# Mixing stage of a fused convolution and Laplace layer: a third tile for the mixed rows, an earlier start of the weights, another form of the exponentials, and another order of the evictions

## The chip, the cores and the metric

The kernel runs on one core of a Trainium2 chip. The metric is the device time of one execution in microseconds; three executions of the kernel before are shown below, and one more was recorded by the profiler. TensorE (PE) multiplies matrices, VectorE (DVE), ScalarE (ACT) and GpSimd (POOL) work on tiles in on-chip memory, and SyncE (SP) issues transfers between that memory and the chip's main memory. Each engine takes its own instructions strictly in the order in which they were written.

## What is computed

The input `x` has 16 images of 16 channels of 256 by 256 points, in 32-bit floats. Two layers follow one another, each of the form x + layer(group norm of x):

```python
x = x + _L0_conv_ref(_gn(x), L0_conv_weight)      # a 3x3 circular convolution
x = x + _L1_conv_ref(_gn(x), L1_conv_ty, ...)     # a Laplace layer
```

The second layer takes the two-dimensional Fourier transform `alpha` of its input. For every frequency pair (o, x) a 16 by 16 matrix of complex numbers mixes the channels, and the result is transformed back. The matrices come from poles and residues:

```python
A = 1.0 / (omega1[:, None, None, None] - weights_pole1[None])
Bm = 1.0 / (omega2[:, None, None, None] - weights_pole2[None])
S = jnp.einsum('ikpq,oikp,xikq->oxik', weights_residue, A, Bm)
output_residue1 = jnp.einsum('biox,oxik->bkox', alpha, S)
```

A second, transient part sums exponentials exp(pole * t) along both axes, with residues `output_residue2` made from `alpha`, `A` and `Bm`. The output is the real part of both parts plus the layer's input.

## The kernel before

The work has four stages, and TensorE is busy in nearly all of each: the convolution (to about 574 us of the profile), the forward transform along lines and columns (to 1193), the mixing of the channels (to 1860) and the transforms back with the output (to the end). The change touches the third stage most; the fourth stage takes over its memory.

In the mixing stage a *group* g (0 to 31) is a set of four frequencies of one axis with all those of the other, and each group has four *places* n. The spectrum lies in main memory as `aD`; the mixed result goes to main memory as `yD`. Per place, in the order in which the loop near line 1222 writes it:

- `sums` (line 1032): 32 small matmuls of the weights `w` with the table `ct` make the mixing matrices of the *next* group into two tiles `ps_s`.
- `spread` (lines 1049 and 1052) brings them to `sg`: for each of the two tiles ScalarE copies one half and VectorE shuffles one half. There are two `sg` tiles, one of this group and one of the next.
- four times `mix` (line 1120): 16 matmuls of `sg` with the spectrum in `abd` make a tile `ps_mix`, which is copied into a quarter of the tile `yt` (line 1233), the first three by ScalarE and the last by VectorE. In a place where `late` is set, VectorE takes two of the four.
- SP's transfers: at place 1 two loads of the next group into `abd01` (line 1102), then always four `store`s of 128 KB each from `yt` to `yD` (line 1134), then the rest of the loads of the next group: at place 1 two more into `abd01` (256 KB each), at places 2 and 3 four of 128 KB each into `abd2` and `abd3` (line 1107), at place 0 none.
- one step of `weights` for the group after next: three steps on VectorE, and with the last the spread of `v` to `w` on POOL (line 930).
- one step of the exponentials `make_exps` (lines 1172 to 1212): for each of 16 pairs of columns POOL works out an angle and brings it into the range of the sine, ScalarE takes exponential and sine, POOL multiplies and folds them, and SP stores the result to `eD`. A pair has seven steps.

There is one `abd` tile per place pair (`abd01`) or place (`abd2`, `abd3`), so a load of the next group waits until the mixes of this one have read it. There are two `yt` tiles, so the copies of one place wait until the stores of the place before the last have landed. All these loads and stores go through SP's one queue. The order of every engine is that of the program text (`manual_schedule`): nothing is reordered.

In group 31 the rows of frequency 0 are taken apart again (`unmix_first`, lines 1139 to 1157), by four loads and four stores of `yD`. Then the fourth stage begins: POOL issues loads of `et`, `ey`, `inv` and of rows 0 to 119 of the mixed result `yk`, SP loads rows 120 to 127 (line 1283), and POOL combines rows into `u` (lines 1325 and 1329), the operand of the first transform back (line 1361).

On-chip memory is laid out by hand: pools in the order in which the stage opens them, with tiles of the fourth stage over those of the third.

Of the kernel before, what the change touches and what calls it, by code (L numbers as in the profile page):

```python
# [9 lines left out]
FP = mybir.dt.float32  # L10
AF = mybir.ActivationFunctionType
# [5 lines left out]
B = 16  # L17
# [7 lines left out]
def conv_then_laplace_kernel(ctx: ExitStack, tc: tile.TileContext, a: dict, out: bass.AP):  # L25
# [25 lines left out]

    later_loads = []

    def const(name, shape):
        t = cp.tile(shape, FP, name=name, tag=name)
        later_loads.append((t, a[name]))
        return t

    cols = const("cols", [P, 24])
    kmask = const("kmask", [P, C])  # L60
    fold2 = const("fold2", [P, 2, 64])
    o2 = cp.tile([P, B, 2, 16], FP, name="o2", tag="o2")
    proj = cp.tile([P, 2, B, 16, 2], FP, name="proj", tag="proj")
    jmat = cp.tile([P, 3, P], FP, name="jmat", tag="jmat")

    def pitched(name, rows, row, *split):

# [27 lines left out]

    ptab = ExitStack()
    tp = ptab.enter_context(tc.tile_pool(name="tables", bufs=1))
    vmr = tp.tile([P, 2, B, C], FP, name="vmr", tag="vmr")


# [54 lines left out]
    own = m16[:, 0:C:2]  # L155
    load_consts()
    halves[1] = [load_x(1, h) for h in range(2)]
    nc.sync.dma_start(out=jmat, in_=a["jmat"])
    ones = tp.tile([P, P], FP, name="ones", tag="ones")
    nc.vector.memset(ones, 1.0)  # L160
    tiny = wp.tile([P, 8], FP, name="tiny", tag="tiny")
# [557 lines left out]
    def pool(stage, name, bufs=1, **kw):  # L719
        return stage.enter_context(tc.tile_pool(name=name, bufs=bufs, reuse_waits="tile", **kw))  # L720
# [174 lines left out]
    def weights(g):  # L895

        shape = [P, 32, 4]
        u = up["u" if g else "u0"].tile([P, 4, 32, 4], FP, name="u", tag="u")  # L900
        w, den, e, f = (u[:, j] for j in range(4))
        pr2, pre, pim = (prU[:, j].unsqueeze(2).to_broadcast(shape) for j in range(3))
        nc.vector.tensor_tensor(
            w,
            omg[:, g].unsqueeze(1).to_broadcast(shape),
            pims.unsqueeze(2).to_broadcast(shape),
            ALU.subtract,
        )
        nc.vector.tensor_tensor(den, w, w, ALU.mult)
        nc.vector.tensor_tensor(den, den, pr2, ALU.add)  # L910
        yield
        nc.vector.reciprocal(den, den)

        nc.vector.scalar_tensor_tensor(e, w, m1, pre, ALU.mult, ALU.add)
        nc.vector.scalar_tensor_tensor(f, w, nm0, pim, ALU.mult, ALU.add)
        yield
        v = up["v"].tile([P, 32, 2, 4], FP, name="v", tag="v")
        nc.vector.tensor_tensor(v[:, :, 0], e, den, ALU.mult)
        nc.vector.tensor_tensor(v[:, :, 1], f, den, ALU.mult)
        if g == 0:  # L920
            yield
        wt = wp.tile([P, 4, 8, 32], FP, name="w", tag="w")
        v2 = v.rearrange("p a r s -> p a (r s)")
        w4 = wt.rearrange("p a k (i m) -> p (a k) i m", i=4)
        if g == 0:
            for i in range(4):
                nc.scalar.activation(w4[:, :, i], v2, AF.Copy, scale=m4[:, i : i + 1])
            return wt
        full = [P, 32, 4, 8]
        nc.gpsimd.tensor_tensor(  # L930
            w4,
            v2.unsqueeze(2).to_broadcast(full),
            m4.unsqueeze(1).unsqueeze(3).to_broadcast(full),
            ALU.mult,
        )
        return wt
# [44 lines left out]
    ptab.close()  # L981


    yp = pool(p2, "yt", 2)
    g0 = pool(p2, "sg0")
    a0 = pool(p2, "abd0")
    wp = pool(p2, "w", 2)
    ep = pool(p2, "exps")
    up["u"] = pool(p2, "u")
    a1 = pool(p2, "abd2")  # L990
    zp = pool(p2, "between")
    tp = pool(p2, "ct")
    a2 = pool(p2, "abd3")
    g1 = pool(p2, "sg1")
# [10 lines left out]
        z.tile([P, 4, 4, 16, B], FP, name=f"abd{j}", tag=f"abd{j}") for j, z in ((2, a1), (3, a2))  # L1005
    ]

    zp.tile([P, 384], FP, name="between", tag="between")
    ct = tp.tile([P, 4, 8, N], FP, name="ct", tag="ct")
    nc.sync.dma_start(out=ct, in_=cD)  # L1010
    def next_step(steps, w):
# [28 lines left out]

    swap = [p ^ 4 for p in range(32)]

    def spread(n, *pairs):


        for odd in range(2):
            for to, src in pairs:
                k = 4 * n + 2 * odd
                nc.scalar.activation(to[..., k : k + 2], src[odd], AF.Copy, scale=nsgn)  # L1049
            for to, src in pairs:  # L1050
                k = 4 * n + 2 * (1 - odd)
                nc.vector.stream_shuffle(to[..., C + k : C + k + 2], src[1 - odd], swap)  # L1052

    def first_sums():
# [27 lines left out]
            load(0, jq)  # L1082
        return sg, w1

    def finish_projections():


        for ro in range(2):
            ps = pm.tile([P, B, 16], FP, name="ps_o", tag="ps_mix")
            nc.tensor.matmul(ps, lhsT=jmat[:, 0], rhs=accs[:, ro], start=True, stop=False)  # L1090
            nc.tensor.matmul(ps, lhsT=jmat[:, 2 - ro], rhs=accs[:, 1 - ro], start=False, stop=True)
            nc.vector.tensor_copy(o2[:, :, ro], ps)

    def load(g, jq, rows=range(4)):

# [65 lines left out]
    def make_exps(which):  # L1161


        pl = ep.tile([P, C, 2], FP, name="s_pl", tag="s_pl")
        nc.sync.dma_start(out=pl, in_=a[f"pole_e{which + 1}"])
        t = ep.tile([P, N], FP, name="s_t", tag="s_t")
        nc.sync.dma_start(out=t, in_=a[("ty", "tx")[which]].to_broadcast([P, N]))
        sign, phase, turns = (cols[:, 2 + 3 * which + j : 3 + 3 * which + j] for j in range(3))
        pim = ep.tile([P, C], FP, name="s_pim", tag="s_pim")
        for _ in range(4):  # L1170
            yield
        nc.gpsimd.tensor_scalar(pim, pl[:, :, 1], sign, None, ALU.mult)
        for q in range(8):
            th = ep.tile([P, 2, N], FP, name="s_th", tag="s_th")
            rn = ep.tile([P, 2, N], FP, name="s_rn", tag="s_rn")
            tmp = ep.tile([P, 2, N], FP, name="s_tmp", tag="s_tmp")
            ex = ep.tile([P, 2, N], FP, name="s_ex", tag="s_ex")
            for j in range(2):
                i = 2 * q + j
                nc.gpsimd.tensor_scalar(th[:, j], t, pim[:, i : i + 1], None, ALU.mult)  # L1180
            nc.gpsimd.tensor_scalar(rn, th, 1.0 / (2 * PI), turns, ALU.mult, ALU.add)
            magic = 1.5 * 2.0**23
            nc.gpsimd.tensor_scalar(rn, rn, magic, None, ALU.add)
            nc.gpsimd.tensor_scalar(rn, rn, magic, None, ALU.subtract)
            yield
            c1 = 6.28125
            c2 = float(np.float32(1.93500518798828125e-3))
            c3 = 2 * np.pi - c1 - c2
            for c in (c1, c2, c3):
                nc.gpsimd.tensor_scalar(tmp, rn, float(c), None, ALU.mult)  # L1190
                nc.gpsimd.tensor_tensor(th, th, tmp, ALU.subtract)
                if c == c2:
                    yield
            nc.gpsimd.tensor_scalar(th, th, phase, 3.1415925, ALU.add, ALU.min)
            nc.gpsimd.tensor_scalar(th, th, -3.1415925, None, ALU.max)
            for j in range(2):
                i = 2 * q + j
                nc.scalar.activation(ex[:, j], t, AF.Exp, scale=pl[:, i, 0:1])
            yield True
            yield  # L1200
            nc.scalar.activation(th, th, AF.Sin)
            yield True
            nc.gpsimd.tensor_tensor(th, th, ex, ALU.mult)
            for op, eo in ((ALU.add, 0), (ALU.subtract, 1)):
                nc.gpsimd.tensor_tensor(
                    ex[:, :, eo * P : eo * P + P], th[:, :, 0:P], th[:, :, N - 1 : P - 1 : -1], op
                )
            yield
            for o in range(2 - which):
                nc.sync.dma_start(  # L1210
                    out=eD[which][o, :, 2 * q : 2 * q + 2].rearrange("p i e t -> p i (e t)"),
                    in_=ex,
                )
            yield
# [1 line left out]
    p2.enter_context(tc.manual_schedule())  # L1216
    accs = yp.tile([P, 2, B, 16], FP, name="accs", tag="yt")
    ahead, wt = first_sums()
    finish_projections()
    unmix = None  # L1220
    exps, late = chain(make_exps(0), make_exps(1)), None
    for g in range(32):
        sg, w_now = ahead, wt
        steps = weights(g + 2) if g < 30 else iter(())
        ahead = new_sg(g + 1) if g < 31 else None
        for n in range(4):
            evict = sums(n, w_now) if ahead is not None else []
            yt = yp.tile([P, 2, 4 * B, 16], FP, name="yt", tag="yt")
            if evict:
                spread(n, (ahead, [z.rearrange("p q n -> p n q") for z in evict]))  # L1230
            for m in range(4):
                o, src = mix(4 * n + m, sg, yt)
                (nc.vector.tensor_copy if m >= (2 if late else 3) else nc.scalar.copy)(o, src)  # L1233
            if n == 1 and g < 31:
# [3 lines left out]
                load(g + 1, n, (2, 3) if n == 1 else range(4))  # L1238
            if n == 1 and unmix is not None:
                next(unmix, None)  # L1240
            wt = next_step(steps, None) or wt
            late = g and next(exps, None)
        if g == 30:
# [210 lines left out]
def _constants():  # L1454
# [45 lines left out]
    cols[:, 6], cols[:, 7] = np.where(even, np.pi / 2, 0), np.where(even, 0.25, 0)  # L1500
    cols[:, 9] = np.where(even, -1.0, 0.0)
    cols[:, 12:16] = p[:, None] // 8 % 4 == np.arange(4)
    cols[:, 17] = p > 0
    cols[:, 16] = -cols[:, 17]
    cols[:, 19] = np.where(p > 0, 1.0, 0.5)
# [104 lines left out]
```

## Time and profile before

| what | value |
|---|---|
| three executions | 2618.83, 2619.7, 2624.65 us; median 2619.7 |
| the profiled execution | 2623.94 us, its span (first to last instruction) 2622.1 us |
| mean granted TensorE clock | 0.986 |
| busy share of the span | PE 94%, weight loads 72%, VectorE 76%, ScalarE 55%, POOL 49% |
| stage 3, 1219 to 1836 us: PE, VectorE, ScalarE, POOL busy | 586.1, 499.8, 400.4, 383.5 of 617 us |
| stage 3: transfers | 16 DMA engines busy 0.77 of the time, 223 GB/s |
| stage 4, 1860 to 2622 us: PE busy | 735.6 of 762 us |

The profile lists for each group of instructions the line, the engine, the operation, the names of the tiles that it writes and reads, its shape and count, then the busy time and the mean duration of one in nanoseconds, then the idle time of the engine just before such instructions and the event that ended most of it. An arrow `<-` reads "from" between tiles and "was ended by" in waits. A number after L is a line of the kernel. A chain of waits follows the work back from an end: each row is a piece of time and what was going on in it. SPq stands for SP's sequencer, and "issue" for time in which nothing that the profile shows was waited for.

### The profile page before, as it was taken

The numbers are of one execution on the slowest core, as the hardware profiler recorded it, in microseconds if no ns is written. First come the engines' busy times: TensorE is split into PE (matmuls) and PEld (weight loads), VectorE is DVE, ScalarE is ACT, GpSimd is POOL, SyncE is SP. The second block draws the span as 40 slices with busy tenths as digits, with TensorE's granted clock in tenths as the row PEclk, the third lists the DMA queues.
The fourth block names the chain that finished last, engine by engine and source line by source line (L and its number), as shares of the span: only waits on it lengthen the run. The fifth ranks groups of instructions, "written<-read, shape, count | busy, mean of one in ns | idle before, by whom it ended". The sixth has DMA issues, their size and how long they took to land.

```text
span 2622.1 us, 84262 instructions
## 1 busy us (share of the span) xinstructions
PE 2468.6 (94%) x35314; PEld 1885.3 (72%) x35314; DVE 1980.8 (76%) x3772; ACT 1432.6 (55%) x2599; POOL 1290.5 (49%) x1179
## 2 busy tenths in 40 slices
PE   5998999989999999998999999999799999999998
PEld 2444455567777777775878778788688888888887
DVE  7777788848888888887877878887276676667666
ACT  2565566666666666665666656666244444444443
POOL 1333378433333333333666645766555565555553
PEclk9999999989999999999999999999899999999999
DMA  7888878854655655655777777777988888888884
GB/s 274 276 279 282 294 270 294 297 211 177 240 195 209 242 220 194 245 225 190 225 229 214 226 225 222 222 227 228 253 302 289 291 292 279 299 289 287 291 287 174
DMA packets 318011, 653.17 MB, mean 249 GB/s; under 512 B 49174, under 2 KB 163990, under 8 KB 305728
## 3 DMA queue, kind: packets, MB, share of 16 engines
q1 hardware_dynamic: 316464, 640.57, 72.4%
q8 instruction: 278, 4.55, 0.7%
q0 software_dynamic: 896, 3.02, 0.4%
q10 hardware_dynamic: 272, 4.19, 0.4%
q14 instruction: 101, 0.83, 0.1%
HBM read 368.15 MB, written 280.36 MB: 247 GB/s over the span
## 4 chain that ended last, share of the span: by engine, by line
PE 58%; DVE 7%; DMA 4%; SPq 3%; ACT 3%; POOL 2%; issue 1%; ACTq 0%; DVEq 0%; POOLq 0%
PE ps_mix L1120 9%; PE ps_y L777 9%; PE ps_y L785 8%; PE ps_p L1361 7%; PE ps_f L1385 7%; PE ps_f L1386 7%; PE ps_x L820 5%; DMA yD<-yt 4%; PE ps_s L1032 2%; SPq L1134 2%; PE ps_h L1345 2%; PE psd L805 1%; DVE r L1394 1%; DVE ol L1396 1%; DVE ol L1397 1%
## 5 line engine op out<-in xcount | busy, mean ns | idle before, releaser
L1120 PE MATMUL ps_mix<-abd,sg 128*64 128x128 f32 x8192 | 482.2, 276 | 39.4 <-DMA yD<-yt 16.6
L1120 PEld LDWEIGHTS ps_mix<-abd,sg 128*64 128x64 f32 x8192 | 451.9, 138 | 92.9 <-ACT yt L1233 55.7
L1325 POOL TENSOR_TENSOR u<-yk 128x512 f32<-128x512 f32 (+1 forms) x268 | 358.2, 1369 | 314.7 <-PE ps_p L1361 249.1
L305 PE MATMUL ps_conv<-xt,wc 32*32 32x512 f32 x12288 | 445.6, 602 | 36.0 <-issue 26.1
L305 PEld LDWEIGHTS ps_conv<-xt,wc 32*32 32x32 f32 x12288 | 251.1, 103 | 217.6 <-issue 127.0
L793 ACT ACTIVATE t<-ps_y,vmr 128x384 f32<-128x384 f32 x512 | 297.1, 580 | 161.1 <-PE ps_y L785 161.1
L1052 DVE STREAM_SHUFFLE sg<-ps_s 128x512 f32<-128x512 f32 (+1 forms) x264 | 329.1, 1316 | 0.0
L777 PE MATMUL ps_y<-tabE,vq 128*128 128x256 f32 x1024 | 313.2, 388 | 11.0 <-DVE vq L766 9.4
L785 PE MATMUL ps_y<-tabO,vq 128*128 128x256 f32 x1024 | 305.9, 380 | 0.0
L275 POOL TENSOR_TENSOR pair<-pair,far 128x1024 f32<-128x1024 f32 x64 | 151.7, 2370 | 304.1 <-DVE pair L272 207.7
L1385 PE MATMUL ps_f<-pt,inv 128*128 128x256 f32 x1008 | 300.4, 380 | 0.0
L1386 PE MATMUL ps_f<-hs,ey 128*128 128x256 f32 x1008 | 299.8, 379 | 0.0
L1361 PEld LDWEIGHTS ps_p<-inv,u 128*128 128x128 f32 x2048 | 268.9, 193 | 35.4 <-POOL u L1329 10.9
L1389 DVE TENSOR_TENSOR r<-ps_f,q 128x256 f32<-128x256 f32 x256 | 107.0, 418 | 241.9 <-ACT q L1388 241.9
L1361 PE MATMUL ps_p<-inv,u 128*128 128x128 f32 x2048 | 276.2, 278 | 9.8 <-POOL u L1329 9.7
L1049 ACT ACTIVATE sg<-ps_s,mcol 128x512 f32<-128x512 f32 (+1 forms) x264 | 179.3, 689 | 192.2 <-DVE sg L1052 117.1
L777 PEld LDWEIGHTS ps_y<-tabE,vq 128*128 128x128 f32 x1024 | 189.6, 191 | 87.5 <-ACT q L833 51.2
L1388 ACT COPY q<-ps_f 128x256 f32<-128x256 f32 x256 | 95.4, 373 | 274.7 <-PE ps_f L1386 250.4
L1363 ACT COPY pt<-ps_p 128x512 f32<-128x512 f32 x256 | 151.5, 592 | 134.9 <-PE ps_p L1361 134.9
L765 POOL TENSOR_TENSOR vq<-vf 128x512 f32<-128x512 f32 x64 | 81.4, 1272 | 291.6 <-DVE vf L769 281.5
L785 PEld LDWEIGHTS ps_y<-tabO,vq 128*128 128x128 f32 x1024 | 195.4, 191 | 26.9
L1233 ACT COPY yt<-ps_mix 128x512 f32<-128x512 f32 x352 | 184.1, 592 | 55.8 <-DMA yD<-yt 42.2
(237 smaller groups left out, 3993.6 us busy)
## 6 DMA issues: line engine op xcount, KB each, us to landing
xt<-in_x SPq DMA_DIRECT2D x288, 258.0 KB
vD<-pair SPq DMA_DIRECT2D x256, 256.0 KB
yD<-yt SPq DMA_DIRECT2D x512, 128.0 KB
vl<-vD SPq DMA_DIRECT2D x128, 512.0 KB
out_y<-ol SPq DMA_DIRECT2D x128, 512.0 KB
s<-vD SPq DMA_DIRECT2D x126, 512.0 KB
aD<-spec SPq DMA_DIRECT2D x15, 4096.0 KB
yk<-yD SPq DMA_DIRECT2D x60, 1024.0 KB
```

Of the source, the lines that this page charges most:

```text
L305: nc.tensor.matmul(acc[r][32 * c : 32 * c + 32], lhsT=ready[b][0][rows, phase, tap], rhs=halves[b][u // 2][rows, q : q + 5 : 4, 2 - tap : ...
L777: nc.tensor.matmul(ps[:, 0:N], lhsT=vf[:, xo, 0, j], rhs=tabE[:, 0 : i + 2 : i + 1], start=True, stop=False, skip_group_check=True,)
L785: nc.tensor.matmul(ps[:, P : P + N], lhsT=vf[:, xo, 1, j], rhs=tabO[:, i : C + 1 : C - i], start=False, stop=True, skip_group_check=True,)
L793: nc.scalar.activation(t[:, xo, j].rearrange("p l n -> p (l n)"), ps[:, 0:384], AF.Copy, scale=vmr[:, 0, b0 + j, i : i + 1],)
L1049: nc.scalar.activation(to[..., k : k + 2], src[odd], AF.Copy, scale=nsgn)
L1052: nc.vector.stream_shuffle(to[..., C + k : C + k + 2], src[1 - odd], swap)
L1120: nc.tensor.matmul(ps[64 * t : 64 * t + 64, j], lhsT=sg[:, f : f + 2].rearrange("p f m -> p (f m)"), rhs=abd[jq][:, :, 2 * t + cc, 2 * jj ...
L1233: (nc.vector.tensor_copy if m >= (2 if late else 3) else nc.scalar.copy)(o, src)
L1325: nc.gpsimd.tensor_tensor(u[:, :, j].rearrange("p b (c n) -> p c b n", c=8), in0, in1, o)
L1361: nc.tensor.matmul(ps[:, at], lhsT=u[:, n], rhs=tab, start=True, stop=True)
L1385: nc.tensor.matmul(ps[:, e], lhsT=tab, rhs=pt[:, e], start=True, stop=False)
L1386: nc.tensor.matmul(ps[:, e], lhsT=ey[:, e], rhs=hs, start=False, stop=True)
```

## The change

In the mixing stage:

- `yt` gets a third tile.
- The steps of `weights(g + 3)` begin at place 3 of group g and go on at places 0 and 1 of the next. Before, `weights(g + 2)` took places 0, 1 and 2 of group g. Weights of group 2 take their first step before the loop.
- ScalarE's order within a place: first half of `sg`, copy of mix 0, second half of `sg`, copy of mix 1, and so on. Before, both halves came ahead of the four copies.
- The exponentials: the angle of a pair of columns is reduced in two halves of 256 columns, addition and subtraction of the magic number are one instruction, and so are minimum and maximum; the phase is no more added on POOL but given to the sine as its bias, with the limits shifted by the phase (four new host constants in `cols`).

Memory for the third tile comes from `kmask` and `fold2` (moved to the pool of tables, which ends before the mixing), `o2` (takes the place of `proj`), `jmat` (takes the place of `s_ex`, loaded at the start of the mixing stage), the removed tile "between", a `u` of three rows in place of four, and `rn` and `tmp` of half the size. SP's order changes for loads of constants alone: these, and three more small ones (`p2k`, `kgrp`, `mcol`), which go from the end of the convolution to its start.

```diff
@@ -51,17 +51,13 @@
-    def const(name, shape):
-        t = cp.tile(shape, FP, name=name, tag=name)
+    def const(name, shape, home=cp):
+        t = home.tile(shape, FP, name=name, tag=name)
         later_loads.append((t, a[name]))
...
     cols = const("cols", [P, 24])
-    kmask = const("kmask", [P, C])
-    fold2 = const("fold2", [P, 2, 64])
-    o2 = cp.tile([P, B, 2, 16], FP, name="o2", tag="o2")
     proj = cp.tile([P, 2, B, 16, 2], FP, name="proj", tag="proj")
-    jmat = cp.tile([P, 3, P], FP, name="jmat", tag="jmat")
@@ -95,6 +91,8 @@
     tp = ptab.enter_context(tc.tile_pool(name="tables", bufs=1))
+    kmask = const("kmask", [P, C], tp)
+    fold2 = const("fold2", [P, 2, 64], tp)
     vmr = tp.tile([P, 2, B, C], FP, name="vmr", tag="vmr")
@@ -155,7 +153,6 @@
     halves[1] = [load_x(1, h) for h in range(2)]
-    nc.sync.dma_start(out=jmat, in_=a["jmat"])
     ones = tp.tile([P, P], FP, name="ones", tag="ones")
@@ -897,8 +894,8 @@
         shape = [P, 32, 4]
-        u = up["u" if g else "u0"].tile([P, 4, 32, 4], FP, name="u", tag="u")
-        w, den, e, f = (u[:, j] for j in range(4))
+        u = up["u" if g else "u0"].tile([P, 3, 32, 4], FP, name="u", tag="u")
+        w, den, e = (u[:, j] for j in range(3))
         pr2, pre, pim = (prU[:, j].unsqueeze(2).to_broadcast(shape) for j in range(3))
@@ -912,11 +909,11 @@
         nc.vector.scalar_tensor_tensor(e, w, m1, pre, ALU.mult, ALU.add)
-        nc.vector.scalar_tensor_tensor(f, w, nm0, pim, ALU.mult, ALU.add)
+        nc.vector.scalar_tensor_tensor(w, w, nm0, pim, ALU.mult, ALU.add)
         yield
...
         nc.vector.tensor_tensor(v[:, :, 0], e, den, ALU.mult)
-        nc.vector.tensor_tensor(v[:, :, 1], f, den, ALU.mult)
+        nc.vector.tensor_tensor(v[:, :, 1], w, den, ALU.mult)
         if g == 0:
@@ -981,14 +978,13 @@
-    yp = pool(p2, "yt", 2)
+    yp = pool(p2, "yt", 3)
     g0 = pool(p2, "sg0")
...
     a1 = pool(p2, "abd2")
-    zp = pool(p2, "between")
     tp = pool(p2, "ct")
@@ -1005,7 +1001,6 @@
-    zp.tile([P, 384], FP, name="between", tag="between")
     ct = tp.tile([P, 4, 8, N], FP, name="ct", tag="ct")
@@ -1040,10 +1035,10 @@
-    def spread(n, *pairs):
-
-
-        for odd in range(2):
+    def spread(n, *pairs, odds=(0, 1)):
+
+
+        for odd in odds:
             for to, src in pairs:
@@ -1082,14 +1077,19 @@
+    jmat = ep.tile([P, 3, P], FP, name="jmat", tag="s_ex")
+    nc.sync.dma_start(out=jmat, in_=a["jmat"])
+
     def finish_projections():
+        o2 = cp.tile([P, B, 2, 16], FP, name="o2", tag="proj")
...
             nc.vector.tensor_copy(o2[:, :, ro], ps)
+        return o2
@@ -1165,6 +1165,7 @@
         nc.sync.dma_start(out=t, in_=a[("ty", "tx")[which]].to_broadcast([P, N]))
+        most, least = (cols[:, j : j + 1] for j in ((8, 10), (11, 18))[which])
         sign, phase, turns = (cols[:, 2 + 3 * which + j : 3 + 3 * which + j] for j in range(3))
@@ -1172,33 +1173,31 @@
             th = ep.tile([P, 2, N], FP, name="s_th", tag="s_th")
-            rn = ep.tile([P, 2, N], FP, name="s_rn", tag="s_rn")
-            tmp = ep.tile([P, 2, N], FP, name="s_tmp", tag="s_tmp")
+            rn = ep.tile([P, N], FP, name="s_rn", tag="s_rn")
+            tmp = ep.tile([P, N], FP, name="s_tmp", tag="s_tmp")
             ex = ep.tile([P, 2, N], FP, name="s_ex", tag="s_ex")
...
                 nc.gpsimd.tensor_scalar(th[:, j], t, pim[:, i : i + 1], None, ALU.mult)
-            nc.gpsimd.tensor_scalar(rn, th, 1.0 / (2 * PI), turns, ALU.mult, ALU.add)
             magic = 1.5 * 2.0**23
-            nc.gpsimd.tensor_scalar(rn, rn, magic, None, ALU.add)
-            nc.gpsimd.tensor_scalar(rn, rn, magic, None, ALU.subtract)
-            yield
             c1 = 6.28125
...
             c3 = 2 * np.pi - c1 - c2
-            for c in (c1, c2, c3):
-                nc.gpsimd.tensor_scalar(tmp, rn, float(c), None, ALU.mult)
-                nc.gpsimd.tensor_tensor(th, th, tmp, ALU.subtract)
-                if c == c2:
-                    yield
-            nc.gpsimd.tensor_scalar(th, th, phase, 3.1415925, ALU.add, ALU.min)
-            nc.gpsimd.tensor_scalar(th, th, -3.1415925, None, ALU.max)
+            for j in range(2):
+                z = th[:, j]
+                nc.gpsimd.tensor_scalar(rn, z, 1.0 / (2 * PI), turns, ALU.mult, ALU.add)
+                nc.gpsimd.tensor_scalar(rn, rn, magic, magic, ALU.add, ALU.subtract)
+                for c in (c1, c2, c3):
+                    nc.gpsimd.tensor_scalar(tmp, rn, float(c), None, ALU.mult)
+                    nc.gpsimd.tensor_tensor(z, z, tmp, ALU.subtract)
+                yield
+            nc.gpsimd.tensor_scalar(th, th, most, least, ALU.min, ALU.max)
             for j in range(2):
...
             yield
-            nc.scalar.activation(th, th, AF.Sin)
+            nc.scalar.activation(th, th, AF.Sin, bias=phase)
             yield True
@@ -1216,19 +1215,21 @@
     ahead, wt = first_sums()
-    finish_projections()
+    o2 = finish_projections()
     unmix = None
...
         sg, w_now = ahead, wt
-        steps = weights(g + 2) if g < 30 else iter(())
+        if g == 0:
+            steps = weights(2)
+            next(steps)
         ahead = new_sg(g + 1) if g < 31 else None
...
             yt = yp.tile([P, 2, 4 * B, 16], FP, name="yt", tag="yt")
-            if evict:
-                spread(n, (ahead, [z.rearrange("p q n -> p n q") for z in evict]))
             for m in range(4):
+                if evict and m < 2:
+                    spread(n, (ahead, [z.rearrange("p q n -> p n q") for z in evict]), odds=(m,))
                 o, src = mix(4 * n + m, sg, yt)
@@ -1238,6 +1239,8 @@
                 next(unmix, None)
+            if n == 3:
+                steps = weights(g + 3) if g < 29 else iter(())
             wt = next_step(steps, None) or wt
@@ -1500,6 +1503,9 @@
     cols[:, 12:16] = p[:, None] // 8 % 4 == np.arange(4)
+    for phase, most, least in ((3, 8, 10), (6, 11, 18)):
+        cols[:, most] = 3.1415925 - cols[:, phase]
+        cols[:, least] = -3.1415925 - cols[:, phase]
     cols[:, 17] = p > 0
```

## The prediction

> **What bounds the kernel now.** I read the groups by line first, to see which wait the mixing stage ends on.
>
> ```profile
> L1120 PE MATMUL ps_mix<-abd,sg 128*64 128x128 f32 x8192 | 482.2, 276 | 39.4 <-DMA yD<-yt 16.6
> L1233 ACT COPY yt<-ps_mix 128x512 f32<-128x512 f32 x352 | 184.1, 592 | 55.8 <-DMA yD<-yt 42.2
> ```
>
> TensorE stands 39.4 us before the mixes, and ScalarE's copies stand 42.2 us for a store of `yt` to land: the wait that a third tile would shorten. Is it the cause? The stretch from the first mix (1219.1 us) to the first mix of group 31 (1835.1) is 616 us for 31 groups. Where TensorE isn't held up, a place (32 sums matmuls in 1.02 us, 64 mix matmuls in 3.64) takes 4.67 us, a group 18.67, so 31 groups need 579: 37 us are lost. Start to start, almost all of it falls between place 3 of a group and place 0 of the next, which take 4.7 to 8.0 us. There the mix needs the new `abd01`. One such gap, in the chain over 1780 to 1803 us and the timeline of SP's queue:
>
> ```profile
> 1791.52 0.58 SPq L1102
> 1792.10 0.04 issue
> 1792.15 5.95 DMA abd<-aD
> 1798.09 0.14 issue
> 1798.23 3.71 PE ps_mix L1120 x64
> ```
>
> ```profile
> 1785.53 2.03 SPq L1134 DMA_DIRECT2D yD<-yt  x4
> 1787.66 1.66 SPq L1102 DMA_DIRECT2D abd<-aD  x2
> 1789.42 2.05 SPq L1134 DMA_DIRECT2D yD<-yt  x4
> 1791.52 1.57 SPq L1102 DMA_DIRECT2D abd<-aD  x2
> 1793.20 2.04 SPq L1134 DMA_DIRECT2D yD<-yt  x4
> 1795.34 3.34 SPq L1107 DMA_DIRECT2D abd<-aD  x4
> ```
>
> The mix starts 0.14 us after its load lands, and SP issues without a pause: each row begins about 0.1 us after the end of the one above. Over the 616 us SP issues 888 DMAs (492 stores, 373 loads, 23 of the tables), 0.694 us each; a group has 28.7 of them, so 19.9 us, more than TensorE's 18.67. SP's queue paces the stage. When I set the end of each tile's copies against the end of SP's issue before its store, SP truly waited 2.3 us for copies in the whole stage, and 2.9 us for mixes before loads: stores begin 5 to 10 us after their mix starts, while the copies are ready after 4.4 to 6.6. Now the waits over the mixing stage (us in total, times, longest):
>
> ```profile
> ACT yt L1233 <- DMA yD<-yt: 26.1, 25, 4.0
> PE ps_mix L1120 <- DMA yD<-yt: 16.6, 12, 3.2
> DVE yt L1233 <- DMA yD<-yt: 15.1, 11, 3.5
> POOL w L930 <- DVE v L919: 177.7, 23, 17.9
> ```
>
> Copies that wait for landings (26.1 + 15.1 us) are what a late SP does to the engines ahead of it; they cost SP only those 2.3 us. POOL stands 177.7 us at the weights: it has room. The last group is different, in the chain from 1835 us:
>
> ```profile
> 1848.72 5.14 DMA yD<-yt
> ...
> 1854.12 0.59 ACT yt L1233
> ...
> 1854.76 5.71 PE ps_mix L1120 x64
> ...
> 1862.62 5.91 DMA yD<-yt
> ...
> 1868.66 2.36 DMA yk<-yD
> ...
> 1871.24 0.20 POOL u L1325
> ```
>
> Here the copies of (31,2) do wait for a tile, and nothing refills SP: store (31,0) lands, copies, mix (31,3), store (31,3), the last rows of `yk`, the first `u`.
>
> **What the Trainium skill says.** "DMA: Bandwidth & Descriptors", section "Anatomy of one DMA", says that a DMA's semaphore wait happens on the issuing sequencer before dispatch: a waiting store holds all behind it on SP. The trace agrees: loads and stores leave in program order. "Runtime: NRT & Kernel Launch", section "Instruction fetch mechanics", calls a 16 KiB refill of instructions mostly hidden. This trace differs: some 95 of SP's issues, one every 6.5 us, are about 1 us longer than the rest and coincide with such fetches (94 packets in the stage). They belong to SP's 19.9 us, and the waits view names a finished engine for many. "GPSIMD Engine Reference", section 3.1, gives a two-input operation 2.6 cycles per element: 1.281 us for 512 against 0.731 for 256 here is 2.15 ns per element plus 0.18 us, which fits at the 1.2 GHz that the page counts with. "TensorE: Matmul & The Clock Gate", Part 1, gives half the rate after an idle window of some 3.4 us: the granted clock is 0.5 from 1848.6 to 1858.8, so mix (31,3) takes 5.71 us instead of 3.7.
>
> **The change, part by part.**
>
> *Third tile, groups 0 to 30.* Removed: the copies' waits for landings. SP's work remains: 888 issues in nearly the same order. What can go is SP's own waits, 5.2 us at most; some follow from late mixes in place 1, which the tile doesn't govern. I take 3.
>
> *Third tile, last group.* Before, the copies of (31,2) began at 1854.1. With a tile free they begin when their mix ends, about 1846.5. Mix (31,3) then runs about 1848 to 1854, if at half clock; its copies end about 1855. SP isn't there before 1857.3 (its issues of the stores (31,0) to (31,2) and the second `unmix` part end near 1857.5, the wait to 1861.3 follows). So store (31,3) is issued 1857.3 to 1859.2 instead of 1861.3 to 1863.4, lands about 1863, and SP's `yk` rows come about 1866 instead of 1871. But POOL's own loads of the other 120 rows, which wait for `unmix` to land (1857.9), landed at 1864.9 and 1867.5, and this edit doesn't move them. First `u`: about 1867.5. Gain 4 us (3 to 5).
>
> *Spread split on ScalarE.* No work added: the copy of mix 0 goes ahead of the second half of `sg`. That half waited for VectorE's first shuffle anyway (ScalarE `sg` for VectorE: 117 us in 97 waits), so the copy fills a hole. It makes `sg` later by one copy (0.59 us) for a mix a group away. TensorE's order is the same. Zero; without the hole, 0.6 us per place on an engine that is busy 400 of 617 us, still hidden.
>
> *Weights one place sooner.* The same three steps on VectorE (1.27, 1.65 and 0.56 us) and one on POOL (1.89 us) per group, in places 3, 0, 1 instead of 0, 1, 2. VectorE (500 of 617 us busy) gets 1.27 us in place 3, less in place 2. Zero; uncovered it would be 1.27 us per group.
>
> *Exponentials.* Per pair of columns, POOL before, up to the sine: 2 × 0.926 + 0.693 + 1.50 + 1.50 + 3 × (1.491 + 1.281) + 2.042 + 1.493 = 17.4 us in 13 instructions, then 1.28 + 2 × 0.73. After: 2 × 0.926, and per half a multiply-add, one two-step addition of the magic number, three multiplications and three subtractions, then one minimum-maximum: 19 instructions. Halves: subtraction 0.731 and multiplication 0.926 from the 256-wide rows; multiply-add 0.35 to 0.69, taken 0.5; magic 0.47 (from 0.693 for a two-step operation of 512 columns) to 2.04, taken 1.0; minimum-maximum with two column pointers 0.69 to 2.04, taken 1.8. Sum 1.85 + 2 × (0.5 + 1.0 + 3 × 1.657) + 1.8 = 16.6 us; with lower bounds for all (half of 1.491 and 1.281 for the three pairs) 12.5, with upper ones 19.3. So "fewer operations" is less arithmetic in more instructions, about 0.8 us less per pair. POOL isn't on the chain here: zero, while it stays within four places (18.67 us at TensorE's pace, 19.9 at SP's) with a weight (1.89) between. Before is 17.4 + 1.9 = 19.3, and ScalarE waited 0.4 us in all at the sine.
>
> *Moved loads and memory.* Two constants and three more small loads change place on SP in the convolution, `jmat` moves in front of the first `abd` loads, where SP stands waiting; about 0, ±1. In the last stage `yk`, `et` and `inv` lie over other tiles; their loads wait for tiles that are free before `unmix` lands. Zero.
>
> Sum on the profiled execution: 2623.9 − 4 − 3 = 2616.9. That execution (span 2622.1 and 1.8 around it) lies 4.2 above the median 2619.7 of the runs shown, so on the median's footing **2613**.
>
> **Rivals.**
>
> *The landing loop was the bound.* For: it is the largest named wait of both copying engines, and 16.6 us of TensorE's. If it goes, groups run at 18.67 us: 37 us lost become about 6 at the refills of `abd01`, −31, and −4 at the end: 2585. Against: SP's rows above have no gap into which earlier copies could put a store.
>
> *Nothing to measure.* SP's waits are filled by its own issues, and the first `u` comes with POOL's `yk`, with TensorE's clock cold as before: −1 to −4, so 2616 to 2619.
>
> *Slower: POOL's chain.* If each instruction on POOL costs more than its length says, the sine's input comes after ScalarE has reached it, and the copies of that place, the stores and the loads behind them on SP are late. Place: 16 sines. It decides from about 22.8 us with the weight (19.9 plus the 3 us by which copies are ahead of SP); my upper bound gives 21.2. At 23.5 it costs 0.7 × 16 = 11 us: with the 4 at the end gained and none of the 3, 2627.
>
> **How the numbers follow.** SP paces and the end gains: 0.52, 2613, own range 2608 to 2617. Landing loop, whole or in part (2585 to 2606): 0.16. Nothing to measure: 0.21. Slower: 0.11. The range 2588 to 2623 leaves out the deepest part of the second case and most of the last. A measurement tells 0.2%, 5.2 us: below 2614.5 counts as faster. That takes two thirds to three quarters of the first case and all of the second, 0.36 + 0.16, so faster 0.52; same 0.37; slower 0.11.
>
> **What would show it.** Right: the copies' waits for `yD<-yt` nearly gone, yet 31 groups in 610 to 616 us, mixes of place 0 starting just after `abd<-aD` lands, SP without gaps; first `u` near 1867 on the old scale; POOL's rows before the sine at 16 to 17 us per pair. Wrong: groups near 18.7 us, or SP's issues shorter in a calmer traffic (second rival); ScalarE waiting at the sine for POOL (last rival); a time changed before 1190 us or after the first `u`, which I hold to be untouched.

## The result and the profile after

Over 14 runs each, the changed kernel has a median of 2624.65 us (2618.11 to 2628.96) and the kernel before 2622.41 us (2612.04 to 2628.02): a ratio of 1.0012, 95% interval 1.0001 to 1.0023. That is 2 or 3 us slower at the most likely and at the edge of what can be told from nothing. The forecast of 2613 us, 7 below the median of the three runs shown of before, was wrong. The profiled execution took 2625.85 us with a span of 2623.9.

The groups by line of the changed kernel, same columns as before. TensorE's idle time before the mixes is the same 39.4 us. Behind ScalarE's copies the profile names landings for 27.7 us in place of 42.2.

```profile
L1120 PE MATMUL ps_mix<-abd,sg 128*64 128x128 f32 x8192 | 477.5, 275 | 39.4 <-DMA yD<-yt 22.5
L1234 ACT COPY yt<-ps_mix 128x512 f32<-128x512 f32 x352 | 200.7, 583 | 78.6 <-DMA yD<-yt 27.7
```

The waits of its mixing stage (us in total, times, longest). VectorE's wait for landings, 15.1 us before, is no longer among the rows: it waits for mixes.

```profile
POOL w L927 <- DVE v L916: 191.2, 26, 16.8
DVE yt L1234 <- PE ps_mix L1120: 91.5, 92, 4.6
ACT yt L1234 <- DMA yD<-yt: 24.1, 42, 2.9
PE ps_mix L1120 <- DMA yD<-yt: 22.5, 16, 3.5
```

The names in the last two rows deceive, as start times in the trace show. All 42 copies of the third row begin 0.08 or 0.09 us after the last matmul of their own mix, so they wait for that mix; before, 24 of the 25 copies named so began later than that, by up to 5.3 us. With three tiles no copy waits for a store any more. The 16 waits of TensorE all stand before the first mix of a place 0, and end 0.24 to 0.38 us after the last load of the new `abd01` landed (before: 12 waits, 0.14 to 0.35 us). They are waits for loads, which no tile for `yt` can shorten.

SP's queue in the timeline, over the same part of the stage as was shown of before: still each row begins about 0.1 us after the end of the one above.

```profile
1789.53 1.99 SPq L1134 DMA_DIRECT2D yD<-yt  x4
1791.62 1.24 SPq L1102 DMA_DIRECT2D abd<-aD  x2
1792.97 2.98 SPq L1134 DMA_DIRECT2D yD<-yt  x4
1796.00 1.23 SPq L1102 DMA_DIRECT2D abd<-aD  x2
1797.34 1.99 SPq L1134 DMA_DIRECT2D yD<-yt  x4
1799.42 3.60 SPq L1107 DMA_DIRECT2D abd<-aD  x4
```

I cut each trace at four points: the start of the convolution's last matmul (its "end" in what follows), the first mix, the first mix of group 31 (the part between these two mixes is the *stretch*: 31 groups), and the first `u` of the last stage.

| trace | convolution ends | to first mix | stretch | to first `u` | to the end |
|---|---|---|---|---|---|
| before | 564.7 | 654.4 | 616.0 | 36.1 | 750.8 |
| changed | 567.8 | 657.2 | 614.4 | 35.2 | 749.3 |
| before, a second trace | 562.0 | 657.6 | 614.3 | 34.6 | 750.9 |

So the two traces of one kernel differ by as much as the two kernels do. In all 16 traces of the experiments the end of the convolution lies anywhere from 558.1 to 570.1 us, with no order by kernel that I could see. The stretch is steadier: 614.4, 613.4, 613.2 and 612.2 for four kernels with the third tile and SP's 28.7 issues per group; 616.0, 614.3, 613.5 and 613.8 for four with `yt` as before, and 619.8 for the changed kernel with two tiles.

Where the time is lost inside the stretch says more. I took the time from the first mix of each place to that of the next, less the 4.67 us of an undisturbed place, summed over the 31 groups (us):

| trace | 0 to 1 | 1 to 2 | 2 to 3 | 3 to next 0 |
|---|---|---|---|---|
| before | 4.8 | 0.0 | 5.3 | 26.7 |
| before, a second trace | 1.6 | 0.6 | 9.4 | 23.5 |
| changed, two tiles (an experiment below) | 2.6 | 1.0 | 5.1 | 32.1 |
| changed | 1.4 | 0.0 | 0.0 | 34.1 |

The third tile removes what was lost in front of place 3, in all four kernels that have it. About as much is lost in front of places 0 and 1 instead (26.2 to 29.3 and 5.2 to 8.0 us in the other three). In front of place 0 the mix waits for loads from SP's queue.

The new end, in the chain of waits from 1840 us, and VectorE's timeline there:

```profile
1850.60 5.04 DMA sg<-yD
...
1858.39 0.69 DVE yt L1234
...
1864.63 7.27 DMA yD<-yt
1872.03 2.45 DMA yk<-yD
...
1874.65 0.18 POOL u L1328
```

```profile
1846.70 0.69 DVE L1234 COPY yt<-ps_mix 128x512 f32<-128x512 f32 x1 [2.80 <-DMA yD<-yt]
1855.77 0.75 DVE L1150 SCALAR_TENSOR_TENSOR sg<-sg,mcol 128x512 f32<-128x512 f32 x1 [8.37 <-DMA sg<-yD]
...
1858.20 0.28 DVE L1155 SCALAR_TENSOR_TENSOR sg<-sg,mcol 128x32 f32<-128x32 f32 x1
1858.39 0.69 DVE L1234 COPY yt<-ps_mix 128x512 f32<-128x512 f32 x1
```

The same two rows of VectorE before, and TensorE's last row of mixes in the changed kernel:

```profile
1852.02 0.27 DVE L1155 SCALAR_TENSOR_TENSOR sg<-sg,mcol 128x32 f32<-128x32 f32 x1
1854.15 0.69 DVE L1233 COPY yt<-ps_mix 128x512 f32<-128x512 f32 x1 [1.86 <-DMA yD<-yt]
```

```profile
1859.13 1.98 PE L1120 MATMUL ps_mix<-abd,sg 128*64 128x128 f32 x16 [4.04 <-DVE yt L1234]
```

With (31,2) I mean place 2 of group 31. VectorE's copy for it stands in its queue behind the arithmetic of `unmix`, which waits for loads of `yD`. ScalarE made its three copies of that place at 1848.3, but the last mix of (31,3) needed the buffer that VectorE freed at 1859.1.

### The profile page after: what moved, and what is told of

Read it like the earlier page. It is cut to its first block, busy times and chain, and to the rows that moved or that the text cites. A ratio compares the mean times of both kernels' runs of the same rounds, so it can differ in the third digit from the quotient of the medians.

```text
span 2623.9 us, 84295 instructions
## 1 busy us (share of the span) xinstructions
PE 2469.8 (94%) x35314; PEld 1887.9 (72%) x35314; DVE 1979.1 (75%) x3772; ACT 1440.6 (55%) x2599; POOL 1262.3 (48%) x1275
## 5 line engine op out<-in xcount | busy, mean ns | idle before, releaser
L1120 PE MATMUL ps_mix<-abd,sg 128*64 128x128 f32 x8192 | 477.5, 275 | 39.4 <-DMA yD<-yt 22.5
L302 PE MATMUL ps_conv<-xt,wc 32*32 32x512 f32 x12288 | 448.2, 609 | 34.1 <-issue 26.4
L1234 ACT COPY yt<-ps_mix 128x512 f32<-128x512 f32 x352 | 200.7, 583 | 78.6 <-DMA yD<-yt 27.7
```

The source lines that it names most:

```text
L302: nc.tensor.matmul(acc[r][32 * c : 32 * c + 32], lhsT=ready[b][0][rows, phase, tap], rhs=halves[b][u // 2][rows, q : q + 5 : 4, 2 - tap : ...
L1120: nc.tensor.matmul(ps[64 * t : 64 * t + 64, j], lhsT=sg[:, f : f + 2].rearrange("p f m -> p (f m)"), rhs=abd[jq][:, :, 2 * t + cc, 2 * jj ...
```

## The experiments

**Does SP's queue pace the stage?** One more transfer of 1 KB per place, for which nobody waits:

```diff
             store(g, n, yt)
+            if g < 31:
+                k = 16 * (4 * g + n)
+                nc.sync.dma_start(out=tick[:, k : k + 16], in_=cols[0:16, 0:16])
```

> The changed kernel with one more DMA of 1 KB on SP in each of the 124 places of groups 0 to 30; it moves next to nothing and nobody waits for it. If SP's queue paces the mixing: each costs its issue, 0.45 to 0.6 us, so the stretch to the first mix of group 31 grows by 50 to 75 us. If the landing of stores or the transfers' bandwidth pace it: by less than 15 us.

Measured: 1.0257 (1.0227 to 1.0287). The stretch is 687.4 us, 73 more for 123 more issues, 0.59 each. In SP's timeline the new one takes 0.44 to 0.45 us here (median of all 0.45), with a pause of about 0.1 us behind it. SP's issue time as a whole grew by 65 of the 73 us:

```profile
1500.70 2.99 SPq L1135 DMA_DIRECT2D yD<-yt  x4
1503.73 0.45 SPq L1241 DMA_DIRECT2D tick<-cols  x1
1504.28 2.81 SPq L1108 DMA_DIRECT2D abd<-aD  x4
1507.20 2.03 SPq L1135 DMA_DIRECT2D yD<-yt  x4
1509.28 0.44 SPq L1241 DMA_DIRECT2D tick<-cols  x1
```

They carry 0.13 MB in all, so it isn't bytes: SP's queue paces, with a cost near the upper end of the 50 to 75 us expected.

**Fewer issues on SP, same bytes.** Two ways. First, the four loads of place 2 issued by ScalarE:

```diff
-                nc.sync.dma_start(
+                (nc.scalar if jq == 2 and g else nc.sync).dma_start(
                     out=abd[jq][s::4, s]
```

> The changed kernel with the four loads of place 2 (abd2, from group 1 on) issued by ScalarE instead of SP: SP has 24.7 issues per group left, some 17.1 us, less than TensorE's 18.67. If SP's queue paces: the stretch goes from 614.4 to 580 to 595 us, the time falls by 20 to 33 us. If transfers or landings pace: it falls by less than 6 us, or rises because ScalarE's copies stand behind its issues (about 0.4 us each, 1.6 us per group).

> The kernel before with the same four loads on ScalarE. If SP's queue hid what a third tile is worth: this gains less than the changed kernel does from the same edit, since copies now wait for landings with SP free; the difference is then the tile's worth with room on SP, 3 to 15 us. If the tile is worth nothing either way: the same gain within 3 us.

Measured: 1.0800 (1.0776 to 1.0824) on the changed kernel, 1.0337 (1.0314 to 1.0361) on the kernel before. Both theories missed. SP's timeline, and one row of ScalarE's, show why:

```profile
1513.67 2.52 SPq L1107 DMA_DIRECT2D abd<-aD  x4
1517.24 1.75 SPq L1134 DMA_DIRECT2D yD<-yt  x4
1529.72 0.58 SPq L1102 DMA_DIRECT2D abd<-aD  x1
```

```profile
1525.81 2.89 ACTq L1107 DMA_DIRECT2D abd<-aD  x4
```

SP stands from 1519.0 to 1529.7, although the mix that it has to wait for ended at 1521.1. In this program every transfer also waits for an earlier one that had the same of eight semaphores, handed round over both queues in program order. So SP now waits for transfers that ScalarE issues late, behind its copies: the wait that ends just before 1529.72 is for the semaphore of the transfer that ScalarE issued at 1525.81. The pauses of SP over 0.2 us sum to 345 us in this stretch, and some 250 us of them end at a semaphore on which ScalarE's transfer was the last one issued. ScalarE's four issues took 2.89 us, not the 1.6 us expected. The two ratios therefore say nothing on the tile. (Where one queue issues all, this wait costs nothing: the transfer eight issues earlier had landed before SP's previous issue ended in all but 4 of 878 cases of the kernel before.)

Second, `abd2` and `abd3` as one tile, loaded by four transfers of 256 KB at place 3 instead of eight of 128 KB at places 2 and 3:

```diff
...
-        if jq == 0:
+        if jq in (0, 2):
             return
+        z = pair if jq == 1 else pair2
...
+                out=z[s::4, s].rearrange("r c h j b -> r c (h j b)"),
+                in_=src[:, :, jq - 1 : jq + 1].rearrange("r c h n -> r c (h n)"),
```

> The changed kernel with abd2 and abd3 in one tile (abd23, after ct in memory), loaded by four DMAs of 256 KB at place 3 instead of eight of 128 KB: the same bytes, 24.7 issues per group on SP instead of 28.7, some 16.9 us instead of 19.8, against TensorE's 18.67. If SP's queue paces: 31 groups in 580 to 598 us instead of 614, time 15 to 33 us below the changed kernel's. If bytes or landings pace: less than 5 us.

> The same with two yt tiles. If a full SP queue is what made the third tile worth nothing: with room on SP the copies wait for landings and delay mixes, 5 to 15 us above the run with three tiles. If the tile is worth nothing in any case: within 3 us of it.

> The kernel before with the same merged loads. If SP's queue paces it as it does the changed kernel: 12 to 33 us faster than before. The other parts of the change (exponentials, spread, weights) then show as the difference to the changed kernel with merged loads and two tiles, which I expect within 3 us.

Measured: 0.9963 (0.9950 to 0.9975) with three tiles, 0.9995 (0.9979 to 1.0011) with two, 1.0009 (0.9996 to 1.0023) on the kernel before. The stretches are 598.0, 600.6 and 607.8 us, against 614.4, 619.8 and 614.3 to 616.0 with eight loads: 16, 19 and 6 to 8 us less. SP's queue is the pace in the kernel before too. But the time doesn't follow: the forecast of 12 to 33 us for the kernel before failed, since from the end of the convolution to the first mix it is now 664.4, 663.3 and 663.6 us, 9 more. I come to that below. What is left in the stretch lies in front of the mixes of place 2 (13.5 us over TensorE's pace), which wait for the merged tile. So the loads of place 3 go ahead of that place's store:

```diff
-            if n == 1 and g < 31:
-                load(g + 1, n, (0, 1))
+            if n % 2 and g < 31:
+                load(g + 1, n, (0, 1) if n == 1 else range(4))
             store(g, n, yt)
...
```

> The changed kernel with merged loads, and at place 3 the four loads ahead of the store. If what is left in the mixes of place 2 (they wait for abd23; 13.5 us over the pace in the run with merged loads) comes from the store issued ahead of these loads: that falls below 5 us, the stretch from 598 to 585 to 592, time 6 to 13 us below the run with merged loads alone. If bytes or landings set it: within 3 us.

Measured: 0.9921 (0.9903 to 0.9939), stretch 582.4 us, 2.0 us over the pace in front of place 2. TensorE's pace alone would give 579, an estimate from 4.67 us per place.

**The tile by itself.** The changed kernel with two `yt` tiles, a blank tile of 8 KB in the third's place:

> The changed kernel with two yt tiles again, all else and all addresses kept. If SP's queue paces the mixing: the stretch from the first mix to the first mix of group 31 goes from 614.4 us to 615 to 619, SP again waits some 5 us for copies and mixes, the time is 0 to 4 us above the changed kernel's. If the third tile gains much and another part of the change eats it: 10 us or more above the changed kernel.

Measured: 1.0012 (1.0002 to 1.0022) to the kernel before, as with three. Stretch 619.8, the longest with SP's 28.7 issues; the first `u` came 38.1 us after it, not 35.2. SP's own waits for copies and mixes are 1.1 us, not the 5 expected. In the groups of this run the profile names landings for 146.8 us of ScalarE's waits before copies, against 27.7 with three tiles:

```profile
L1235 ACT COPY yt<-ps_mix 128x512 f32<-128x512 f32 x352 | 196.5, 589 | 187.7 <-DMA yD<-yt 146.8
```

Here nearly all of these copies do begin well after their own mix has ended (by 2.0 us in the median). So the third tile takes at least 119 us of waits away, and what time that saves is too little for these intervals to tell. This trace has it at 5 us in the stretch, the other kernels with two tiles at 1 to 2.

**The other parts one by one.** Old order of the spread, and the weights in their old place, each in the changed kernel:

> The changed kernel with both halves of sg ahead of the four copies on ScalarE, as before. If the split spread costs nothing on a path that SP paces: stretch from the first mix to the first mix of group 31 within 2 us of the changed kernel's 614, time within 2 us. If the split gives back what the tile gains (ScalarE's copies now interleave with its sg halves): 2 to 6 us faster than the changed kernel.

> The changed kernel with the weights in places 0, 1 and 2 again. If the earlier place costs nothing: stretch and time within 2 us of the changed kernel's. If POOL's or VectorE's queue is worse off with it (the exponentials stand behind the weights): 2 to 6 us faster.

Measured: 1.0008 (0.9998 to 1.0018) and 1.0002 (0.9991 to 1.0013), stretches 613.2 and 612.2: neither part can be told from the changed kernel's 1.0012. The new exponentials alone, in the kernel before:

> The kernel before with the new form of the exponentials alone (limits shifted by the phase, the phase as bias of the sine). If POOL isn't on the path: stretch within 2 us of 616, time within 2 us of before. If the new form delays SP's stores of the tables or ScalarE's sine: stretch 618 to 622, time 2 to 6 us above before.

Measured: 1.0036 (1.0021 to 1.0052), 9 us slower, with a stretch of 613.5, shorter than before. Neither theory: what grew lies ahead of the mixing. The chain there:

```profile
1187.62 15.37 DMA ct<-cD
1202.99 0.14 issue
1203.13 3.16 PE ps_s L1032 x49
```

The first sums wait for the table `ct`, and SP issued it at 1187.62, after the last matmuls of the stage before and 629 us after the end of the convolution; in the second trace of before it left at 1171.43, 609 us after. The halved `rn` and `tmp` moved all tiles behind them down by 2 KB, and it seems that `ct` so came to lie over a tile that is read to the end of the forward transform. The same edit with 2 KB of room, which leaves addresses as they were:

```diff
-    zp.tile([P, 384], FP, name="between", tag="between")
+    zp.tile([P, 896], FP, name="between", tag="between")
```

> The kernel before with the new exponentials and 2 KB of room beside them, so that all addresses after them are those of before. If the 9 us that the new form cost alone came from ct's lower address (first sums 12 us later after the end of the convolution): within 2 us of before. If they came from the instructions on POOL or ScalarE: again 6 to 10 us slower.

Measured: 1.0004 (0.9992 to 1.0017). The 9 us were the address. The 9 us of the merged loads look like the same thing: there `ct` lay 16 KB lower, and TensorE stood 16.0 us for it (in the run with earlier loads). The last version below tests it.

**The end.** The second part of `unmix` one place later, behind the copies and the store of (31,2):

```diff
-            if n == 1 and unmix is not None:
+            if n == 2 and unmix is not None:
```

> The changed kernel with the second part of unmix in place 2 of group 31 instead of place 1, behind the copies and the store of that place on VectorE and SP. If VectorE's copy of the last mix of (31,2), behind unmix in the queue, is what held the last mix: mix (31,3) follows (31,2) without the 4.0 us gap, the last store is issued 3 to 6 us earlier against the first mix of group 31, the time falls by 1 to 4 us. If the loads of POOL's yk rows, behind the stores of unmix, bound the first u anyway: the last mixes move, the first u does not, the time stays within 1 us.

Measured: 1.0007 (0.9993 to 1.0021). The mixes end 14.4 us after the first of group 31 instead of 21.7, the last store lands at 26.4 instead of 32.5: the reading of VectorE's queue is right. But the rows of `yk` now take 10.85 us, in the chain:

```profile
1851.57 2.18 DMA yD<-yt
1853.74 1.23 POOL yk L1286
1854.97 10.85 DMA yk<-yD
...
1865.90 0.87 POOL u L1328 x2
```

POOL starts its first two operations of `u` at 1861.8 and the next at 1865.9, 37.0 us after the first mix of group 31, where the changed kernel has 35.2. POOL's second load of `yk` landed 36.9 us after the first mix of group 31, against 33.8 in the changed kernel and 32.4 before. Stores that land six us sooner buy nothing: the second of the two expectations holds.

**A version that beats both.** With `ct` in two tiles the first half keeps the old address; only the second, needed later, lies over the late tile:

```diff
+    ct = [z.tile([P, 4, 4, N], FP, name="ct", tag="ct") for z in tp]
+    nc.sync.dma_start(out=ct[0], in_=cD[:, :, 0:4])
...
+    nc.sync.dma_start(out=ct[1], in_=cD[:, :, 4:8])
```

> The changed kernel with merged loads, the four loads of place 3 ahead of its store, and ct in two tiles so that its first half keeps its old address (with ct 16 KB lower, the first sums came 12 us later). If that late start is an address that is free too late: the first mix comes 8 to 10 us sooner against the end of the convolution than in the run with merged loads, and the time falls by as much, to 26 to 32 us below before. If the start is set elsewhere: within 3 us of the run with merged and earlier loads.

> The same with two yt tiles. If the third tile's worth was hidden by SP's queue: 4 to 12 us slower than with three, the copies' waits for landings back. If SP with room empties two tiles in time: within 2 us.

Measured: 0.9884 (0.9863 to 0.9905), 2590.78 us against 2621.94, with a stretch of 580.3 us and 658.1 us from the end of the convolution to the first mix (663.8 with merged and earlier loads alone). That is 5.7 us sooner, less than the 8 to 10 expected; the trace with two tiles has 655.3. With two tiles 0.9890 (0.9868 to 0.9913), stretch 588.7. The groups of the version with three tiles, and its SP:

```profile
L1114 PE MATMUL ps_mix<-abd,sg 128*64 128x128 f32 x8192 | 475.9, 274 | 7.9 <-DVE yt L1228 5.6
```

```profile
1503.43 5.05 SPq L1128 DMA_DIRECT2D yD<-yt  x8
1510.13 1.51 SPq L1100 DMA_DIRECT2D abd<-aD  x2
1511.75 2.04 SPq L1128 DMA_DIRECT2D yD<-yt  x4
1513.83 1.48 SPq L1100 DMA_DIRECT2D abd<-aD  x2
```

TensorE's idle time before the mixes is 7.9 us instead of 39.4, and SP pauses (1508.5 to 1510.1). What the third tile is worth here stays open: two traces differ by 8.4 us in the stretch, the times by 0.06% with intervals of ±0.2%; with merged loads alone it was 0.32%, with intervals that just miss each other. Some gain of 0 to 8 us fits both.

**The scatter.** The kernel before, a second time:

> The kernel before itself once more, for the scatter of stages between two executions: end of the convolution, stretch, tail. Time within 2 us of before. If the stretch comes out within 2 us of 616, stretches of single traces can be compared to 2 us; if it scatters as the end of the convolution does (558 to 568 in the traces so far), differences below 5 us in one trace say nothing.

Measured: 1.0000 (0.9984 to 1.0015); its stages are in the table above. The stretches of these two traces agree to 2 us, the ends of the convolution to 3, and over all kernels these ends scatter by 12.

## Why the prediction was wrong

*SP's queue paces the mixing stage.* Right, and shown from both sides: 0.59 us more per issue added, 16 to 19 us less in the stretch with four issues per group fewer (6 to 8 on the kernel before), 32 to 34 less when the last loads also go ahead of a store. So the first rival, the landing loop as the bound (copies wait for stores, stores for copies), is refuted: its waits on ScalarE fell by at least 119 us through the tile alone, at unchanged time. The prediction's sign for this, the copies' waits nearly gone, came true. Its reading that almost all of the loss falls in front of place 0 was too strong: it is 27 of 37 us.

*Third tile, groups 0 to 30: "I take 3".* This term was mis-sized, and rested on one trace. SP's own waits for copies and mixes, from which the 3 us were to come, are 5.2 us before and 0.7 us in the changed kernel by the same reckoning; but they are 0.5 us in the second trace of before and 1.1 us in the changed kernel with two tiles, so the 5.2 belonged to that execution and the fall to 0.7 isn't the tile's. What the tile did remove, the loss in front of place 3, came back in front of places 0 and 1. The four traces with three tiles have stretches some 1 us shorter on the mean than the four with `yt` as before, less than one kernel scatters; SP's issues sum to 552 us in the trace before, 557 in its second trace and 558 in the changed kernel.

*Third tile, last group: "with a tile free they begin when their mix ends".* This step failed, and with it the 4 us. The free tile isn't the only thing that the copies of (31,2) need. VectorE's one stands behind `unmix`, which ended 17.2 us after the first mix of group 31 before and 19.0 us after it in the changed kernel, because its last load took 5.0 us to land (3.0 before); why, stays open. Counted from the same mix, the last store was issued 2.3 us sooner and landed 7.27 instead of 5.91 us later: at 32.5 us, against 33.4 and 31.8 in the two traces of before. The first `u` came at 35.2 us instead of 36.1 (34.6 in the second trace). The prediction named POOL's load of `yk` as a bound at 1867.5, but counted it as fixed; it waits for the stores of `unmix`, and its second part landed 33.8 us after that mix, not 32.4. With `unmix` out of VectorE's way the mixes ended 7.3 us sooner and this load landed at 36.9, so the 4 us weren't there even then.

*The footing.* I took 4.2 us off because the profiled execution lay so far above the median of the three runs shown. Over 14 runs the median of before is 2622.41, and that execution lay 1.5 above it. This alone made the forecast 2.7 us too low. A median of three runs with a spread of 6 us can't carry a correction of 4.

*Exponentials: zero.* Right (1.0004 with addresses kept), and the price was near. POOL's rows by shape in the changed kernel's mixing stage:

```profile
L1191 POOL TENSOR_SCALAR s_tmp<-s_rn 128x256 f32<-128x256 f32 x96 | 82.6, 860 | 8.3
L1189 POOL TENSOR_SCALAR s_rn<-s_rn 128x256 f32<-128x256 f32 x32 | 34.7, 1085 | 2.7
L1188 POOL TENSOR_SCALAR s_rn<-s_th,cols 128x256 f32<-128x256 f32 x32 | 15.3, 479 | 3.3
L1194 POOL TENSOR_SCALAR s_th<-s_th,cols 128x512 f32<-128x512 f32 x16 | 12.7, 791 | 1.4
```

With 0.919 for an angle and 0.733 for a subtraction, a pair of columns takes 2 × 0.919 + 2 × (0.479 + 1.085 + 3 × 1.593) + 0.791 = 15.3 us to the sine, where I took 16.6. The minimum-maximum at 0.79 against a taken 1.8 is most of the difference. ScalarE doesn't wait at the sine, so the slower rival (a POOL chain past 22.8 us) was far off.

*Spread, weights, start of the mixing: zero.* Right within what can be told. Counted from the end of the convolution the first sums came 2 to 4 us later, behind ScalarE's four copies to `w`, and that is made up before the first mix: 654.4 to 654.9 us in five other kernels of the same layout, 657.2 in the changed kernel's own trace, 657.6 in the second trace of before.

Put together, the traces give some 1 us less in the stretch, nothing at the end and nothing at the start. The measured time is 3 us more, interval 0.3 to 6. The two meet only at the interval's edge. The small loads that moved to the start of the convolution don't explain it: its end lies at 563.1 us on the mean of the twelve traces with them moved and at 563.3 in the six without, with means good to about 2 us. The four variants of the changed kernel in which one part was taken back or moved also lie above 1, at 1.0002 to 1.0012, so a small cost is likelier than none; where it lies stays open. Of the cases, "nothing to measure", at a chance of 0.21, came nearest by its mechanism. The number of the slower case, 2627, lies nearer to 2624.65, but only by chance: its POOL chain played no part.

## What to carry to other kernels

A wait that tops a profile may be the slack in front of a full queue: before giving it a buffer, compare the issues per round of the one queue in the loop, times their mean duration, with the round of the busiest engine; if the queue is longer, a buffer moves the wait elsewhere, and what helped here was fewer, larger transfers in a better order. Before trusting a wait's name, set its end against the end of the work that the instruction needs. Take the end of a stage apart on every engine, not just along the chain: the instruction that waits next is often one that stands in the same queue behind something unrelated. And when an edit changes a tile's size, look at what comes to lie over what: here 2 KB cost 9 us, some three times the difference between the two kernels.

## What was not expected

- A second issuing queue made it worse by 8% (3.4% on the kernel before), since in this program transfers of both queues share semaphores in turn and the early queue waits for the late one.
- A tiny transfer (1 KB) costs SP a median of 0.45 us of issue, as much as a store of 128 KB (0.45); a load of 256 KB costs what one of 128 KB does (medians 0.604 and 0.603).
- On POOL the number of steps in an operation doesn't set its price: 256 columns take 0.479 us for multiply-add with a column pointer, 0.860 for one multiplication by a constant, 1.085 for adding and subtracting constants; 512 columns take 0.791 for minimum-maximum with two column pointers, and took 2.042 for add-minimum with one.
